# A four-layer model on one core: score constants built on many rows at once, the first search's preparations stepped inside it, layer 2's combine paced, and layer 3's weights loaded during layer 2

## The chip, the cores and the metric

The kernel runs on one core of a Trainium2 chip. The metric is the device time of one execution in microseconds (us); lower is better. All arithmetic is in 32-bit floats. The core has TensorE (PE, matrix products into PSUM, with a separate row PEld for its weight loads), VectorE (DVE), ScalarE (ACT), GpSimd (POOL), and SyncE (SP), whose queue issues most DMAs.

## The reference

Input and output are 8 sequences (b) of 512 tokens of 128 numbers. Four layers follow one another; each is an attention-like part and a feed-forward part (ffn), each added to a running x after a normalisation.

- Layer 0: differential attention, 16 heads of 8 with two score maps each (m = 0 and 1), a causal mask and a per-head linear position bias; beside it a mixture of 4 routed experts (2 chosen by a softmax gate) and 2 shared ones.
- Layer 1: softmax attention for the queries whose greatest score stands out most from their mean score, and a routed mixture of many small experts.
- Layer 2: a gated delta rule (a linear attention with a state per head, in blocks of 32 tokens, with short convolutions ahead of it) beside a mixture of experts whose tokens are gathered by expert.
- Layer 3: softmax attention with a relative position bias, beside a gated ffn whose weights come as integers to be divided by 127.

Of layer 0, what the change touches is this:

```python
bias = slopes[None, :, None, None] * pos_diff[None, None, :, :]
causal = jnp.where(jnp.triu(jnp.ones((s, s), bool), 1), -jnp.inf, 0.0)[None, None]
s0 = jnp.einsum('bhqd,bhkd->bhqk', q0, k0) * scale - bias + causal
s1 = jnp.einsum('bhqd,bhkd->bhqk', q1, k1) * scale - bias + causal
w0 = jax.nn.softmax(s0, axis=-1)
w1 = jax.nn.softmax(s1, axis=-1)
```

## The kernel before, in words

**Order.** TensorE's order is written out by hand: the stages are Python generators, and `step(gen)` lets one go on by one yield, `drain` to its end. The order of the other engines' instructions, and of SP's queue, is made by a scheduler that works with simulated times of its own and keeps to the data's dependencies. Every tile belongs to a pool; a tag with `bufs=n` cycles through n buffers, and a new tile waits until the old one's readers are done. A pool that is opened where a closed one lay waits for all of the old one's tiles there.

**Layer 0.** `score_rows` (L377) makes the constant rows of the score product. K and Q tiles `KA[i][m][g]` and `QA[i][m][g]` (two buffers i, for alternating batches; two maps m; four head groups g) have four groups of 32 rows, one per head. In each group rows 0 to 7 are the head's q or k, row 8 is the negated greatest score, and the following rows carry position bias and a causal mask inside a block, so that one product of 32 rows gives the biased score. Before, 18 such rows are built one at a time: a k row for eight heads and a q row, each made by POOL in one of two ping-pong buffers (tags "flat" and "nmT", L402 to L415), scaled by the slope on DVE, and sent by two small DMAs to the DRAM tiles `l0kc` and `l0qc` (L416, L417). From there 20 DMAs fill the master tiles QA[0][0][0] and KA[0][0][g] (L420, L424), and 27 copies on ACT and DVE (L431) fill the others.

`attention0_inputs(b)` (L435) normalises x, transposes it and makes q, k and v; q and k go through the buffers "flat" to DRAM (L452), and `attention0_loads(b, i)` (L461, DMAs L468) brings head pair i back into rows 0 to 7 by 8 DMAs. `gate0` (L612) is the softmax gate, of five steps, whose last writes the weights to DRAM (`wd`, L626) for `ffn0` (L629) to spread over the partitions as C (L636). An ffn step multiplies by the first weights (`ph`), applies ACT, multiplies by C on POOL (L649), and two steps later multiplies by the second weights into `po`; the first addend of `po` is a bias product with the gate's transposed weights. `attention0_greatest(b)` (L472) is the search for each row's greatest score: 8 head pairs of 6 steps (r = 0 to 47); per step, score products into PSUM and DVE's fused reductions (L500); once per pair a transpose (`pmx`, L481), a negation on ACT and a small DMA to row 8. The values (products with exponentiated scores) follow the search.

At the start, `layers01` (L217) drains batch 0's inputs, all its loads, batch 1's inputs and loads, and both gates; then it runs the first search with one ffn step on every odd r (24 steps).

**Layer 2** (`layer2`, L1027). A unit u is one block of 128 tokens of four of the sequences; 8 units in all, each of 12 rounds. In each unit `rounds` interleaves the delta rule's stages on TensorE: `delta_front` (L1403: window copies nb, convolution outputs y, the transposes byt and chan, products), `delta_inverse` (L1489), which makes two products, AT and PT, of 32-column blocks (256 small matmuls on 32 by 32 tiles, then two DVE multiplications by the decay factors E, L1504), and inverts a triangular matrix by repeated products pY and flips TM (L1525); `delta_scan` (L1597) carries the state; `delta_output` (L1637). The experts (`experts2`, L1313) run beside units 0 to 3. From unit 4 on, `combine2` (L1369) goes on by one step per round: for one finished unit at a time it gathers each token's two expert outputs by indirect DMAs that POOL issues (L1311), sums them on DVE (L1384, L1391), adds the delta rule's output and adds the result to x on POOL (L1394). Tiles nb1, y, byt, chan1, AT, TM, Y, gl and E lie in layer 2's own pool `wk`.

**Layer 3** (`layer3`, L1682) opens new pools where layer 2's lay, loads Wv, Wq, Wk, the bias and Wo, scales Wq on POOL (L1692), and transposes three integer weights (`dequantised`, L1909: a DMA, a cast and a scaling on DVE L1917/L1918, three transposes L1921, an evacuation) ahead of the first transposed norm. Then it runs 64 groups of scores (DVE L1784), softmax, values and ffn.

Of the kernel before, what the change touches and what calls it, by code (L numbers as in the profile page):

```python
# [16 lines left out]
P = 128  # L17
# [14 lines left out]
def tile_kernel(ctx: ExitStack, tc: tile.TileContext, w: dict, out: bass.AP):  # L32
# [7 lines left out]
    fw = sm2 = None  # L40
# [176 lines left out]
    def layers01():  # L217

        nonlocal wk
        with ExitStack() as lx:  # L220
# [5 lines left out]
            with tc.manual_schedule(engines={mybir.EngineType.PE}):  # L226
                for b in range(2):
                    drain(attention0_inputs(b, c))
                    for i in range(8):
                        attention0_loads(b, i, c)  # L230
# [3 lines left out]
                drain(gate0(0, c), gate0(1, c))  # L234
                ffn = ffn0(c)
                for r, _ in enumerate(attention0_greatest(0, c)):
                    if r % 2:
                        step(ffn)
                done = iter(())
# [137 lines left out]
    def score_rows(lp, dram):  # L377

        KA, QA = ([[[lp.tile([P, S], F32, name=f"l0{n}A{i}{m}{g}") for g in range(4)] for m in range(2)] for i in range(2)]
                  for n in "kq")
        row = lp.tile([1, H8], F32, name="l0slr")
        for h in range(H8):
            V.memset(row[:, h : h + 1], 2.0 ** (-8.0 * (h + 1) / H8))
        sd = dram.tile([H8, 1], F32, name="l0sd", bufs=1)
        nc.sync.dma_start(sd.rearrange("h o -> o h"), row)
        slope = lp.tile([H8, 1], F32, name="l0slope")  # L390
        nc.sync.dma_start(slope, sd)
        n = 18
        kc = dram.tile([H8, n, S], F32, name="l0kc", bufs=1)
        qc = dram.tile([n, S], F32, name="l0qc", bufs=1)
        for r in range(n):
            t = wk.tile([H8, S], F32, tag="flat", name=f"l0kc{r}")
            q = wk.tile([1, S], F32, tag="nmT", name=f"l0qc{r}")
            if r == 0:
                G.memset(t, 1.0)
                G.memset(q, 0.0)  # L400
            elif r < 5:
                G.iota(t, pattern=[[P, NT], [0, P]], base=-P * (r - 1), channel_multiplier=0, allow_small_or_imprecise_dtypes=True)  # L402
                G.memset(q, 0.0)
                G.memset(q[:, (r - 1) * P : r * P], 1.0)
            elif r == 5:
                G.iota(t, pattern=[[0, NT], [1, P]], base=-64, channel_multiplier=0, allow_small_or_imprecise_dtypes=True)
                G.memset(q, 1.0)
            else:
                k, i = divmod(r - 6, 3)
                G.memset(t, 0.0)  # L410
                G.memset(t[:, k * P + 32 * (i + 1) : k * P + 32 * (i + 2)], 1.0)
                G.memset(q, 0.0)
                G.memset(q[:, k * P : k * P + 32 * (i + 1)], -30000.0)
            if 1 <= r <= 5:
                V.tensor_scalar(t, t, slope, None, ALU.mult)  # L415
            nc.sync.dma_start(kc[:, r, :], t)  # L416
            nc.sync.dma_start(qc[r : r + 1, :], q)  # L417
        V.memset(QA[0][0][0], 0.0)
        for j in range(4):
            nc.sync.dma_start(QA[0][0][0][32 * j + 8 : 32 * j + 8 + n, :], qc)  # L420
        for g in range(4):
            V.memset(KA[0][0][g], 0.0)
            for j in range(4):
                nc.sync.dma_start(KA[0][0][g][32 * j + 8 : 32 * j + 8 + n, :], kc[4 * j + g])  # L424
        at = 0
        for i in range(2):
            for m in range(2):
                for g in range(4):
                    for X, src in ((KA, KA[0][0][g]), (QA, QA[0][0][0])):
                        if X[i][m][g] is not src:  # L430
                            (A.copy, V.tensor_copy)[at % 2](X[i][m][g], src)  # L431
                            at += 1
        return KA, QA, qc[0:1, :].rearrange("o n -> (o n)").partition_broadcast(4)
# [593 lines left out]
    def layer2():  # L1027
        nonlocal wk, fw, sm2
        with ExitStack() as lx:
# [9 lines left out]
            with tc.manual_schedule(engines={mybir.EngineType.PE}):  # L1039
# [4 lines left out]
                out = iter(())  # L1044

                def rounds(u, experts, combined, n_experts):
                    nonlocal out
                    scan = delta_scan(u, c)
                    inverse = delta_inverse(u + 1, c) if u + 1 < N else iter(())
                    front = delta_front(u + 2, c) if u + 2 < N else iter(())  # L1050
                    for r in range(12):
                        step(scan)
                        step(experts)
                        if not u and r > 1:
                            step(experts)
                        step(inverse)
                        if r > 1:
                            step(front)
                        if r % 3 < n_experts:
                            step(experts)  # L1060
                        step(out)
                        if u > 3:
                            step(combined)
                    drain(scan, inverse, front, out)
                    out = delta_output(u, c)
# [10 lines left out]
                with tc.tile_pool(name="ex2", bufs=1) as ep:  # L1076
                    experts = experts2(ep, c)
                    combined = combine2(ep, c)
                    for u in range(1, N):
                        rounds(u, experts, combined, 1)  # L1080
                    drain(out, experts, combined)
# [321 lines left out]
    def delta_front(u, c):  # L1403
# [20 lines left out]
        for back in range(4):  # L1424
            x = wk.tile([P, 4, P], F32, tag=f"nb{back}", name=f"nb{back}{nm}", bufs=1 if back else 4)
# [13 lines left out]
        y = wk.tile([P, 4, S], F32, tag="y", name=f"y{nm}", bufs=1)  # L1439
# [35 lines left out]
        for i, parts in enumerate((((0, None, G), (1, gam, V)), ((0, beta, G), (1, None, V)))):  # L1475
            byt = wk.tile([P, 2, 4, 4, 32], F32, tag="byt", name=f"byt{i}{nm}", bufs=1)
            for k, part in enumerate(parts):
                scaled(byt[:, k], *part)
            x = wk.tile([P, 2, 4, 4, 32], F32, tag=f"chan{i}", name=f"chan{i}{nm}", bufs=1 if i else 3)
# [9 lines left out]
    def delta_inverse(u, c):  # L1489
# [7 lines left out]
        prod = []  # L1497
        for i, n in enumerate(("AT", "PT")):
            pp = psS.tile([P, 4, 4, 32], F32, tag="S", name=f"p{n}{nm}")
            for ch in range(4):  # L1500
                for h in range(4):
                    tiles32(pp[:, ch, h, :], r["KT"][:, ch, h, :], chan[1][:, i, ch, h, :])
            x = wk.tile([P, 16, 32], F32, tag=n, name=f"{n}{nm}", bufs=1 + i)
            V.tensor_tensor(x, pp.rearrange("p c h i -> p (c h) i"), E, ALU.mult)  # L1504
            prod.append(x)
            yield
        AT, r["PT"] = prod
# [15 lines left out]
        def flipped(n):  # L1523
            x = wk.tile([P, 16, 32], F32, tag="TM", name=f"TM{nm}_{n}", bufs=1)
            V.transpose(x.rearrange("p n i -> p (n i)"), TT.rearrange("p n i -> p (n i)"))  # L1525
            return x
# [3 lines left out]
        for n in range(1, 5):  # L1530
# [3 lines left out]
            Y = wk.tile([P, 16, 32], F32, tag="Y", name=f"Y{nm}_{n}", bufs=1)  # L1534
# [51 lines left out]
    def decay_pairs(u, g, c):  # L1586

        gl = wk.tile([P, 16, 32], F32, tag="gl", name=f"gl{u}", bufs=1)
# [3 lines left out]
        E = wk.tile([P, 16, 32], F32, tag="E", name=f"E{u}", bufs=1)  # L1592
# [89 lines left out]
    def layer3():  # L1682
        nonlocal wk
        with ExitStack() as lx:
            lp = lx.enter_context(tc.tile_pool(name="l3", bufs=1))
            wk = lx.enter_context(tc.tile_pool(name="wk3", bufs=2))
            c = dict(lp=lp, xnT={}, v={}, qk={}, P={}, PT={}, th={}, s={})
            for n in "vqk":
                c["w" + n] = loaded(lp, [P, 1024], w[f"L3_attn_W{n}"], f"l3w{n}")
            c["bias"] = position_bias(lp, shared["bias"])  # L1690
            c["wo"] = loaded(lp, [P, 8, D], w["L3_attn_Wo"].rearrange("(g p) o -> p g o", p=P), "l3wo")
            G.tensor_scalar(c["wq"], c["wq"], 1.0 / 64.0, 0.0, ALU.mult, ALU.add)  # L1692
# [7 lines left out]
            c["gT"], c["uT"], c["dT"] = (dequantised(lp, w[f"L3_ffn_w_{n}"], n) for n in ("gate", "up", "down"))  # L1700
# [208 lines left out]
    def dequantised(pool, src, name):  # L1909

        raw = pool.tile([P, 3, P], I32, tag="rawi", name=f"rawi{name}")
        if src.shape[0] == P:
            nc.sync.dma_start(raw, src.rearrange("o (c p) -> o c p", p=P))
        else:
            nc.sync.dma_start(raw, src.rearrange("(c p) d -> p c d", p=P))
        f = pool.tile([P, 3, P], F32, tag="rawf", name=f"rawf{name}")
        V.tensor_copy(f, raw)  # L1917
        V.tensor_scalar(f, f, 1.0 / 127.0, None, ALU.mult)  # L1918
        pt = psS.tile([P, S], F32, tag="S", name=f"pti{name}")
        for k in range(3):  # L1920
            T.transpose(pt[:, k * P : (k + 1) * P], f[:, k, :], ident)  # L1921
        dst = pool.tile([P, 3, P], F32, name=f"l3{name}")
        evac(dst, pt[:, 0 : 3 * P].rearrange("p (c o) -> p c o", o=P))
        return dst

    with tc.tile_pool(name="x12", bufs=1) as x12:
        with tc.tile_pool(name="fw", bufs=8) as fw:
            layers01()
        layer2()
    layer3()  # L1930


# [21 lines left out]
```

## Time and profile before

| | us |
|---|---|
| three timed runs | 4029.34, 4039.8 (median), 4045.39 |
| the profiled execution | 4008.45 |
| its span in the profile | 4006.7 |
| TensorE busy in it | 3580.8 (89%) |
| DVE / ACT / POOL busy | 2268.1 / 1831.8 / 1470.8 |
| mean granted TensorE clock | 0.933 |
| first score product of layer 0 | 69.68 |
| first rhs of the delta rule's units 0 to 7 | 2509.1, 2611.6, 2698.1, 2779.5, 2861.6, 2979.3, 3062.5, 3122.6 |
| last addition to x in layer 2, first softmax input of layer 3 | 3168.61, 3204.72 |

The profile's page and the trace come from one profiled execution; its times run from the span's start. The page gives busy time by engine, the span in 40 slices of about 100 us with each engine's busy tenths, and the TensorE clock that was granted in tenths of full speed. Timelines list runs of like instructions, with the idle time of the engine before them and what ended it in square brackets. The table of waits sums such idle times by what was waited for. The table of windows gives busy time and counts by engine for chosen stretches.

### The profile page before, as it was taken

The numbers are of one execution on the slowest core, as the hardware profiler recorded it, in microseconds if no ns is written. First come the engines' busy times: TensorE is split into PE (matmuls) and PEld (weight loads), VectorE is DVE, ScalarE is ACT, GpSimd is POOL, SyncE is SP. The second block draws the span as 40 slices with busy tenths as digits, with TensorE's granted clock in tenths as the row PEclk, the third lists the DMA queues.
The fourth block names the chain that finished last, engine by engine and source line by source line (L and its number), as shares of the span: only waits on it lengthen the run. The fifth ranks groups of instructions, "written<-read, shape, count | busy, mean of one in ns | idle before, by whom it ended". The sixth has DMA issues, their size and how long they took to land. (4 is left out here: it accounts for less than half of the span.)

```text
span 4006.7 us, 87035 instructions
## 1 busy us (share of the span) xinstructions
PE 3580.8 (89%) x33646; PEld 1712.2 (43%) x33646; DVE 2268.1 (57%) x7301; ACT 1831.8 (46%) x3996; POOL 1470.8 (37%) x2122
## 2 busy tenths in 40 slices
PE   3899999999999999999999985788947599999998
PEld 1343344444344333333333333456635355555555
DVE  4655666665655544446446646544454466666665
ACT  1254454455454556565664641122211155555554
POOL 2233334334443333332333333444373133333333
PEclk6999999999999999999999987899967699999999
DMA  3000000000011232222222320011020200000000
GB/s 110 29 23 30 28 13 30 30 18 26 26 44 51 75 104 72 80 73 72 71 75 68 81 75 28 11 42 51 28 51 22 63 1 4 4 4 4 4 4 6
DMA packets 139420, 163.29 MB, mean 41 GB/s; under 512 B 30047, under 2 KB 79878, under 8 KB 138880
## 3 DMA queue, kind: packets, MB, share of 16 engines
q1 hardware_dynamic: 135680, 150.91, 13.2%
q0 software_dynamic: 3328, 6.82, 1.0%
q8 instruction: 266, 4.36, 0.5%
q14 instruction: 146, 1.20, 0.1%
HBM read 129.94 MB, written 30.08 MB: 40 GB/s over the span
## 5 line engine op out<-in xcount | busy, mean ns | idle before, releaser
L500 DVE CUSTOM_DVE_ANT_0 l0junk<-ps,l0junk 128x512 f32<-128x512 f32 (+3 forms) x1024 | 502.2, 490 | 394.1 <-PE ps L82 319.6
L985 POOL TENSOR_TENSOR h<-h,C 128x512 f32<-128x512 f32 x256 | 325.2, 1271 | 640.1 <-ACT h L983 587.0
L556 ACT ACTIVATE PT<-pt 128x512 f32<-128x512 f32 (+1 forms) x768 | 360.9, 524 | 404.7 <-PE ps L82 364.2
L807 DVE TENSOR_REDUCE nm<-ps 128x1 f32<-128x512 f32 x512 | 331.7, 685 | 327.2 <-PE ps L82 326.2
L1791 POOL TENSOR_SCALAR P<-P,l 128x128 f32<-128x128 f32 (+3 forms) x512 | 262.8, 532 | 537.8 <-DVE l L1789 382.4
L1788 ACT ACTIVATE P<-P,mx 128x128 f32<-128x128 f32 (+3 forms) x512 | 281.2, 550 | 300.0 <-DVE mx L1786 296.5
L82 PE MATMUL ps<-l0kA,l0qA 32*128 32x512 f32 (+3 forms) x2048 | 403.8, 479 | 11.4 <-DVE mx L500 11.4
L560 POOL TENSOR_SCALAR_AFFINE_SELECT PT<-PT 128x256 f32<-128x256 f32 x512 | 202.0, 407 | 518.9 <-ACT PT L556 486.7
L82 PE MATMUL pt<-l0qA,l0kA 32*128 32x512 f32 (+3 forms) x2048 | 373.2, 468 | 2.0 <-DVE nm L807 1.1
L82 PE MATMUL ps<-l1kA,l1qA 32*128 32x512 f32 x1024 | 332.0, 652 | 29.0 <-DVE nm L807 26.7
L845 ACT ACTIVATE PT<-pt 128x512 f32<-128x512 f32 x512 | 276.3, 595 | 176.0 <-PE ps L82 146.3
L82 PE MATMUL av<-PT,vl0v 128*9 128x512 f32 (+3 forms) x3072 | 319.4, 504 | 1.2 <-POOL PT L560 1.2
L82 PE MATMUL ph<-xnT,l1e 128*128 128x512 f32 x512 | 295.4, 660 | 7.2 <-DVE H L834 2.7
L982 ACT ACTIVATE h<-ph 128x512 f32<-128x512 f32 x272 | 162.8, 599 | 252.6 <-PE ph L82 227.0
L82 PE MATMUL pt<-l1qA,l1kA 32*128 32x512 f32 x1024 | 273.6, 644 | 1.0 <-DVE nm L807 1.0
L82 PE MATMUL po<-h,l1e 128*128 128x512 f32 x512 | 266.5, 602 | 0.0
L82 PEld LDWEIGHTS pt<-l0qA,l0kA 32*128 32x128 f32 x2048 | 165.3, 184 | 206.8 <-DVE mx L500 66.9
L1784 DVE CUSTOM_DVE_ANT_0 P<-ps,l3bias 128x128 f32<-128x128 f32 (+3 forms) x512 | 225.0, 486 | 41.2 <-PE ps L82 39.4
L649 POOL TENSOR_TENSOR h<-h,C 128x512 f32<-128x512 f32 x128 | 163.0, 1274 | 112.3 <-ACT h L647 64.3
L647 ACT ACTIVATE h<-ph,l0b 128x512 f32<-128x512 f32 x192 | 132.0, 687 | 127.6 <-PE ph L82 127.5
L82 PEld LDWEIGHTS ps<-l0kA,l0qA 32*128 32x128 f32 x2048 | 158.3, 187 | 48.3 <-DVE mx L500 34.7
L82 PE MATMUL ps<-kT,qT 64*128 64x128 f32 (+3 forms) x1024 | 176.0, 456 | 1.2 <-ACT kT L77 0.7
(522 smaller groups left out, 6424.5 us busy)
## 6 DMA issues: line engine op xcount, KB each, us to landing
C<-wd SPq DMA_DIRECT2D x288, 256.0 KB
qd<-qf SPq DMA_DIRECT2D x24, 256.0 KB
kd<-kf SPq DMA_DIRECT2D x24, 256.0 KB
l0qA<-qd SPq DMA_DIRECT2D x256, 16.0 KB
l0kA<-kd SPq DMA_DIRECT2D x256, 16.0 KB
l2e<-in_L_ffn_w_dram SPq DMA_DIRECT2D x16, 256.0 KB
l3flat<-l3short SPq DMA_DIRECT2D x16, 192.0 KB
l2eo_d<-eo SPq DMA_DIRECT2D x8, 320.0 KB
```

What stands on the lines that cost most here:

```text
L82: T.matmul(out_, lhsT, rhs, start=start, stop=stop)
L500: V.tensor_tensor_reduce(c["junk"][:, : (qb + 1) * P], pss[j][:, at], c["mask"][:, (3 - qb) * P :], 1.0, NEG, ALU.add, ALU.max, mx[i][:, q ...
L556: A.activation(p[:, j % 2, :N], pss[j][:, :N], AF.Exp)
L560: G.affine_select(out=own, in_=own, compare_op=ALU.is_ge, fill=0.0, base=0, pattern=[[0, 2], [1, P]], channel_multiplier=-1)
L649: G.tensor_tensor(h, h, C[b, e], ALU.mult)
L807: V.tensor_reduce(nm[g][:, j, qb : qb + 1], pss[j], AX.X, ALU.max, negate=True)
L845: A.activation(Pt[j // 2][:, j % 2, :], pss[j], AF.Exp)
L982: A.activation(h, ph, AF.Relu)
L985: G.tensor_tensor(h, h, C[b, u - u % 2][:, u % 2, :], ALU.mult)
L1784: V.tensor_tensor_reduce(p, src, c["bias"][:, 2 * g + j, (3 - qb) * P :], 1.0, NEG, ALU.add, ALU.max, mx[:, n : n + 1])
L1788: A.activation(p, p, AF.Exp, bias=mx[:, n : n + 1], accum_out=l[:, n : n + 1])
L1791: G.tensor_scalar(p, p, l[:, n : n + 1], 1.0, ALU.mult, ALU.mult)
```

## The change

Four parts.

(a) `score_rows` now makes 22 constant rows (16 mask rows where there were 12), built on many rows at once with memsets, iotas and affine selects, and sent to DRAM by 7 DMAs. The master tiles are QA[1][1][0] and KA[1][1][g], and the copies go to buffer 0 first.

(b) The start of `layers01` drains only batch 0's inputs and three of its loads. Gate 0, the other five loads, batch 1's inputs, its loads and its gate become steps of the first search, at the values of r that the diff shows; ffn steps run at r of 16 and more, on three of four (again 24).

(c) In layer 2 the combine is stepped on odd rounds only. A pool `wk23` (`wf`), opened below layer 2's pools and kept through layer 3, holds nb1, y, byt, chan1, AT, TM, Y, gl and E. AT and PT come from two halves of 64-column matmuls with four half multiplications.

(d) `weights3` is stepped in unit 7: it loads layer 3's Wv, Wq, Wk, Wo and the three integer weights into those tiles' buffers, scales, casts and transposes them. Layer 3 itself then only loads the bias and bo.

```diff
             with tc.manual_schedule(engines={mybir.EngineType.PE}):
-                for b in range(2):
-                    drain(attention0_inputs(b, c))
-                    for i in range(8):
-                        attention0_loads(b, i, c)
+                drain(attention0_inputs(0, c))
+                for i in range(3):
+                    attention0_loads(0, i, c)
...
-                drain(gate0(0, c), gate0(1, c))
-                ffn = ffn0(c)
+                ffn, gate, inputs, gate_1 = ffn0(c), gate0(0, c), attention0_inputs(1, c), gate0(1, c)
                 for r, _ in enumerate(attention0_greatest(0, c)):
-                    if r % 2:
+                    if r % 3 == 0 and r < 15:
+                        step(gate)
+                    if r % 2 == 0 and r < 10:
+                        attention0_loads(0, 3 + r // 2, c)
+                    if 16 <= r < 24:
+                        step(inputs)
+                    elif r % 2 == 0 and r >= 26 and r < 42:
+                        attention0_loads(1, (r - 26) // 2, c)
+                    if r % 4 == 0 and r >= 28:
+                        step(gate_1)
+                    if r >= 16 and r % 4 != 3:
                         step(ffn)
+                drain(gate, inputs, gate_1)
...
-        n = 18
+        n = 22
...
-        for r in range(n):
-            t = wk.tile([H8, S], F32, tag="flat", name=f"l0kc{r}")
-            q = wk.tile([1, S], F32, tag="nmT", name=f"l0qc{r}")
...
-            nc.sync.dma_start(kc[:, r, :], t)
-            nc.sync.dma_start(qc[r : r + 1, :], q)
...
+        t = wk.tile([H8, S], F32, tag="flat", name="l0kw")
+        G.memset(t, 1.0)
+        kept(t, [[1, S]], -32, -32)
+        kept(t, [[-1, S]], 63, 32)
+        nc.sync.dma_start(kc[:, 6:n, :].rearrange("h r n -> r h n"), bcast(t, 1, H8))
...
+        for i in range(2):
+            iota(two[1 + i], [[-P, 2], [P, NT], [0, P]], -2 * P * i)
+            V.tensor_scalar(two[1 + i], two[1 + i], slope, None, ALU.mult)
+            nc.sync.dma_start(kc[:, 1 + 2 * i : 3 + 2 * i, :], two[1 + i])
...
+                weights = weights3()
...
-                        if u > 3:
+                        if u > 3 and r % 2:
                             step(combined)
+                        if u == N - 1:
+                            step(weights)
...
-                    drain(out, experts, combined)
+                    drain(out, experts, combined, weights)
...
+        AT = wf.tile([P, 16, 32], F32, tag="AT", name=f"AT{nm}")
+        r["PT"] = wk.tile([P, 16, 32], F32, tag="PT", name=f"PT{nm}", bufs=2)
+        for half in range(2):
+            pp = psS.tile([P, 8, 2, 32], F32, tag="S", name=f"pAP{nm}_{half}")
+            for n in range(8):
+                ch, h = divmod(8 * half + n, 4)
+                tiles32(pp[:, n, :, :], r["KT"][:, ch, h, :], chan[1][:, :, ch, h, :])
+            at = slice(8 * half, 8 * half + 8)
+            for i, x in enumerate((AT, r["PT"])):
+                V.tensor_tensor(x[:, at, :], pp[:, :, i, :], E[:, at, :], ALU.mult)
+            yield
...
+    def weights3():
+        c = shared["w3"] = {}
+        two = wf.tile([P, 2, 1024], F32, tag="y", name="l3wvq")
+        c["wv"], c["wq"] = two[:, 0, :], two[:, 1, :]
+        c["wk"] = wf.tile([P, 1024], F32, tag="byt", name="l3wk")
+        for n in "vqk":
+            nc.sync.dma_start(c["w" + n], w[f"L3_attn_W{n}"])
+        c["wo"] = loaded(wf, [P, 8, D], w["L3_attn_Wo"].rearrange("(g p) o -> p g o", p=P), "l3wo", tag="chan1")
...
+        yield
+        G.tensor_scalar(c["wq"], c["wq"], 1.0 / 64.0, 0.0, ALU.mult, ALU.add)
+        for _ in range(3):
+            yield
+        for raw, (n, key, _, tag) in zip(raws, names):
+            V.tensor_copy(raw, raw.bitcast(I32))
+            V.tensor_scalar(raw, raw, 1.0 / 127.0, None, ALU.mult)
+            yield
...
-        layer2()
-    layer3()
+        with tc.tile_pool(name="wk23", bufs=1) as wf:
+            layer2()
+            layer3()
```

## The prediction

> **What bounds the kernel now.** I read the page's busy shares first, then its 40 slices (the TensorE row and its clock row), because the change touches only a few stages of a 4007 us span.
>
> ```profile
> span 4006.7 us, 87035 instructions
> ...
> PE   3899999999999999999999985788947599999998
> ...
> PEclk6999999999999999999999987899967699999999
> ```
>
> TensorE (PE) is at nine tenths or more almost everywhere. What is left lies in the first slices (0 to 200 us), in slices 24 to 32 (2400 to 3200 us), and nowhere else. The table of windows agrees: from 200 to 2390 us TensorE has 2104.71 of 2190 us. Three views then show the three places.
>
> Start, TensorE's timeline (columns: start, busy, engine, line, what, in brackets the idle time before it and its releaser):
>
> ```profile
> 44.56 2.08 PE L82 MATMUL pq<-xnT,l0wq 128*128 128x512 f32 x2 [11.30 <-ACT qf L448]
> ...
> 69.68 2.80 PE L82 MATMUL ps<-l0kA,l0qA 32*128 32x512 f32 x8
> ...
> 83.90 2.07 PE L82 MATMUL po<-wT,l0b 6*128 6x512 f32 x2
> 114.12 2.07 PE L82 MATMUL po<-h,l0r 128*128 128x512 f32 x2 [28.15 <-POOL h L649]
> ```
>
> The first scores start at 69.68, and at 85.97 TensorE stops for 28 us, for a product of GpSimd (POOL). The table of waits from 30 to 126 us says what POOL wanted: "POOL h L649 <- DMA C<-wd: 42.8". SP's timeline says why C is late: the gate's row wd is sent at 107.74, behind batch 1's eight loads (85.63 to 107.7), 64 DMAs of about 0.33 us each.
>
> Layer 2's valley, busy time and granted clock by windows, and two waits from 2897 to 2998:
>
> ```profile
> 2850.00:2900.00 50.00, 44.83 (x1352) 35.55 (x1353) 27.55 (x78) 13.01 (x32) 20.86 (x26) 0.90 0.10 29
> 2900.00:2950.00 50.00, 23.73 (x584) 14.66 (x582) 20.30 (x49) 4.76 (x12) 40.51 (x47) 0.72 0.28 71
> 2950.00:3000.00 50.00, 22.80 (x840) 16.78 (x840) 31.53 (x74) 6.21 (x12) 38.75 (x37) 0.57 0.26 31
> ```
> ```profile
> DVE g L1384 <- DMA g<-l2eo_d,l2row: 28.1, 7, 6.6
> ...
> PE pY L82 <- DVE TM L1525: 20.5, 2, 12.7
> ```
>
> The first four numbers after the length are PE, weight loads, VectorE (DVE) and ScalarE (ACT), the fifth is POOL. Before the valley PE has 45 of 50 us; in it PE has 23 and POOL 40. POOL issues gathers (L1311) back to back, one per 1.25 us; DVE stands in its queue behind combine's wait for their data, and the delta rule's flips (TM) stand behind that on DVE.
>
> Layer 2 to 3, table of waits from 3168 to 3206:
>
> ```profile
> PE ptigate L1921 <- DVE rawfgate L1918: 24.0, 1, 24.0
> ```
>
> Layer 3's transposes of a weight that was only requested at 3178.35 stand ahead of its first norm in PE's order. The last x is ready at 3168.61, the first softmax input is read (L1784) at 3204.72: 36.1 us.
>
> **Start, constants.** Removed: 36 row DMAs of 0.22 to 0.45 us that SP issues from 14.48 to 44.40 among others, and the POOL/DMA ping-pong over two buffers, which also holds qf (ACT idle 13.24 us, "<-POOL l0kc L410"). Added: 7 DMAs, about 7 × 0.3 = 2 us of SP, and a dozen POOL and DVE operations of 1 us or less (estimate from POOL's 0.4 us L560 select on 256 columns). The slope's round trip stays (requested 14.08 and 18.43), so kc is there about 23 and the 20 master loads (1.36 + 5.65 us of SP) issue by about 31. The 27 copies of about 0.53 us on two engines remain (7.4 us), and the instruction order puts them ahead of batch 0's first xnT evacuation: projections at 33 to 40, at half clock (1.04 us each matmul of 512). Only three of eight loads (8 DMAs, 2.6 us each) precede the first scores: about 46 instead of 69.68.
>
> **Start, search.** Full-clock rows of 120 to 192 give a head pair: PE 1.07+1.65+1.37 scores, 0.44 transpose, about 0.2 of gaps: 4.75 us; an ffn step 1.92; DVE 9.7 (6 × 0.69 and its smaller forms, 16 reductions of 0.08). Steps 0 to 15 are 2.67 pairs without ffn, so DVE is the bound: 2.67 × 9.7 = 26, plus 3 for the gate's small DVE work: to 75. Steps 16 to 47: 5.33 × 4.75 = 25.3; 24 ffn steps × 1.92 = 46.1; batch 1's inputs 5.3; its gate and bits 2.8: 79.5. Moved with the gate: its wd and C DMAs; at about step 13 they pass loads 3 to 7 (40 DMAs, 13 us of SP, spread over 26), but C stands behind one search row and one qd store on SP, each waiting for work of steps 16 to 18. I put 5 us there, the length of such a round trip by Wq's 5.1 us from issue to use, and 3.5 for clock steps. End: 75 + 79.5 + 8.5 = 163. Before, values start at 192.2. **Gain 28**, bounds 18 (C waits twice as long and first scores 5 later) and 36 (neither stall).
>
> **Clock, row against rule.** The windows give 69.68 to 85.97: PE 16.09 of 16.29 us busy at a granted clock of 0.50, whereas 114.12 to 120.00, 5.88 us busy, was followed by 0.99. My 79.5 us are at full clock. The Trainium skill (TensorE: Matmul & The Clock Gate, What's actually happening) says that one busy window of about 3.4 us releases the clock. By that rule all 79.5 us run full; by the first row they may not. The row disagrees with the rule, the second agrees, and the difference is the third rival's price.
>
> **Layer 1 to 2.** The first bias load now waits for s1sb of batch 7 (2403) where it waited for PE at 2390; its norm at 2409.4 stays. 0 to 1 us lost.
>
> **Layer 2, products.** pAT and pPT were 256 matmuls of 32 columns a unit; pY's 128 such take 1.25 us, so 2.5. Now 128 of 64 columns; 32 of those take 0.47 (pu), so 1.88: 0.6 us × 8 = 5, minus four DVE halves in place of two products of 0.69 (about +0.3 a unit), with some issue gaps saved. AT comes one round later. **Gain 4**, 0 to 8.
>
> **Layer 2, pacing.** Combine steps only on odd rounds from unit 4. In the instruction order, 22 gathers still stand in one row on POOL right after unit 5's decay product gl. But until unit 7's window copies (nb) POOL now has 48 gathers and 12 x-additions instead of 56 and 16: 8 × 1.25 + 4 × 0.42 = 11.7 us less. These come later, over unit 7, where POOL is 14 of 50 to 68 us busy, with 4 us of new stall. **Gain 8**, 0 (the row of 22 is what stalls) to 40 (of the valley's 50 us of PE stalls, 12.69 + 10.12 + 7.82 + 3.65 + the rest, all but the gather waits' ends go).
>
> **Layer 3's weights.** Four loads and three raw ones, about 4.9 us of SP, move into unit 7, behind unit 4's expert sum loads and ahead of unit 5's s store: none waits there for anything unfinished. POOL's scaling (1.07 us) waits for Wq: 5.1 us from issue to use at 3168.64, behind it unit 6's and 7's Vb and state. Plus six DVE operations of 0.36, three evacuations of 0.5, nine transposes (2.7). Unit 7's PE is 38 of 68 us busy, so part hides. **Cost 2**, 0 to 6 (the whole Wq wait uncovered).
>
> **Boundary.** Gone from PE's order ahead of ptxnT: the 24.0 us wait and three transposes. What is late next: xn, which DVE writes at 3172.95 to 3173.88, behind four bias memsets of 0.91 (their buffer, a new pool's, still waits for layer 2's last addition). So ptxnT ends about 3174.4 and not 3191.9. The bias load (3170.06 plus 2.88) lands about 3177 and is wanted about 3187. **Gain 17.5**, 14 to 20. Layer 3 and layers 0 and 1 after 200 us keep their work.
>
> **Sum**: 28 − 1 + 4 + 8 − 2 + 17.5 = 54.5 on a profiled execution of 4008.45 us (span 4006.7). The three timed runs have a median of 4039.8, 31.4 above it; none of the edits touches what differs, so the difference counts from there: 4039.8 − 55 = **3985**.
>
> **Rivals.**
> (1) *The valley opens.* For: every stall there ends in DVE or POOL work behind a gather. Against: 22 gathers stay in a row. Gain 32 more: about 3953. Chance 0.12.
> (2) *The start pays half and the valley nothing*: ffn waits for C again, now behind the search's rows on SP, as it waited before. Gain 18 (start) + 3 (products) + 15 (boundary) − 4 (weights) = 32: 4008. Chance 0.17.
> (3) *The clock stays at 0.50 through steps 16 to 47*, for its row above, against the rows from 120 on. The 79.5 us then take 159: search ends at 242, 50 later than before. With 15 from the boundary, 4 from the products, nothing in the valley and 4 for the weights: 4039.8 + 50 − 15 = 4075, slower. Without it the start gains 28 and these 15: it decides once 43 of the 79.5 us (54%) run at half clock. Chance 0.05.
> (4) *The change doesn't do what it says*: the planner's order puts the loads, gathers and weights so that each wait only moves (first scores still near 70, the first layer 3 input still 36 us after x). About 4030. Chance 0.08.
> My forecast keeps 0.58, spread 3965 to 4003.
>
> A measurement here tells about 0.5% (20 us) from no change. Faster by more: forecast, (1) and (2), 0.87 less the tail of (2) near 4020: 0.85. Within: (4) and part of (2): 0.11. Slower: (3) less its mild part: 0.04. The range takes the forecast, (2) and most of (1): 3948 to 4014.
>
> **What would show it.** In the profile after: first scores near 46; TensorE without an idle time of 20 us or more before 150, with clock 1.0 from about 80; values from about 163; combined products in 1.9 us a unit at full clock; units 4 to 6 of layer 2 shorter by 8 in sum while POOL's row of gathers remains; softmax input about 18 us after the last x. The prediction is wrong if C's wait ends later than 90 us, if Wq's scaling delays a state in unit 7 by more than 6 us, or if stages outside these move.

## The result, and the profile after

The changed kernel takes 3981.95 us (median of four runs, 3977.89 to 3987.41) beside 4034.66 for the kernel before: ratio 0.9867, 95% interval 0.984 to 0.9894, or 53 us less. The forecast was 3985. Its profiled execution is one of the four runs (3987.41 us, span 3985.7). Times of runs below are medians; one run of the kernel before (4648.91) and one of warm_all (6557.68), far above all others of their kernel, are not counted.

The two profiled executions differ by only 21 us of span, though, not 53. From the two traces, stage by stage (us from the first to the next mark):

| stage | before | after |
|---|---|---|
| to layer 0's first scores | 69.7 | 47.0 |
| first scores to first values (the search) | 122.5 | 126.4 |
| values to the end of layer 1 | 2197.6 | 2202.3 |
| end of layer 1 to layer 2's first rhs | 119.3 | 124.3 |
| first rhs of unit 0 to that of unit 7 | 613.5 | 619.1 |
| unit 7 to the last combine sum | 43.6 | 43.7 |
| last combine sum to layer 3's first softmax input | 38.5 | 21.3 |
| rest | 802.0 | 801.5 |

So the boundary did what was forecast (17 us), the start gave 18.8 us up to the values where 28 were forecast, and layer 2, whose terms were to bring 12 us, looks 6 us longer. Either the change loses there, or the trace of before is not typical. That was the first question for the experiments.

Page of the profile after:

```profile
span 3985.7 us, 84887 instructions
...
PE   5999999999999999999999975689957699999998
...
PEclk7999999999999999999999987789967799999999
```

Counted from 0, slice 0 has risen from 3 to 5 and slice 31, with the boundary in it, from 5 to 6; layer 2 (slices 24 to 31) still holds the low figures. 2148 instructions are gone, almost all of them by the merged products (1024 matmuls and as many weight loads).

TensorE's timeline of the start after:

```profile
47.00 2.35 PE L82 MATMUL ps<-l0kA,l0qA 32*128 32x512 f32 x4 [5.80 <-DMA l0kA<-kd]
...
51.08 14.44 PE L82 MATMUL ps<-l0kA,l0qA 32*128 32x512 f32 x52
...
78.16 2.08 PE L82 MATMUL ph<-xnT,l0r 128*128 128x512 f32 x2
...
94.95 2.07 PE L82 MATMUL po<-h,l0r 128*128 128x512 f32 x2 [4.22 <-POOL h L669]
```

First scores at 47.0 (forecast 46), the 28 us wait for C down to 4.22 (forecast 5). But from 47 on, four windows (length, then busy time of PE, weight loads, DVE, ACT, POOL, then the granted clock) show another cost:

```profile
47.00:78.00 31.00, 30.84 (x112) 17.41 (x112) 22.25 (x91) 1.39 (x3) 0.98 (x4) 0.50 0.20 57
78.00:90.70 12.70, 12.70 (x24) 4.22 (x22) 6.37 (x29) 3.24 (x5) 0.00 (x0) 0.55 0.06 23
94.95:107.40 12.45, 12.45 (x22) 4.13 (x22) 3.82 (x13) 1.28 (x2) 2.39 (x2) 0.54 0.15 52
107.40:173.00 65.60, 64.71 (x269) 26.32 (x269) 38.16 (x155) 17.95 (x28) 17.42 (x17) 1.00 0.15 41
```

TensorE is busy for all but 0.2 of 43.7 us at a granted clock of 0.50 to 0.55. The boundary, from the table of waits from 3162 to 3206, has lost the 24.0 us wait for a weight to be transposed; what is left is a wait for the first norm:

```profile
PE ptxnT L125 <- DVE xn L118: 12.8, 1, 12.8
```

### The profile page after: what moved, and what is told of

The parts are those of the page before. It is cut to its first block, busy times and chain, and to the rows that moved or that the text cites. A ratio compares the mean times of both kernels' runs of the same rounds, so it can differ in the third digit from the quotient of the medians.

```text
span 3985.7 us, 84887 instructions
## 1 busy us (share of the span) xinstructions
PE 3612.3 (91%) x32622; PEld 1727.2 (43%) x32622; DVE 2261.6 (57%) x7315; ACT 1832.8 (46%) x3996; POOL 1459.5 (37%) x2072
## 4 chain that ended last, share of the span: by engine, by line
PE 75%; DVE 12%; issue 4%; POOL 3%; ACT 3%; DMA 1%; SPq 1%; POOLq 0%; DVEq 0%; ACTq 0%
PE ph L82 12%; PE pt L82 12%; PE po L82 10%; PE av L82 10%; PE ps L82 7%; PE ptp L1819 3%; PE py L82 3%; PE pk L82 2%; PE s L82 2%; PE pq L82 2%; ACT P L1806 2%; PE pv L82 2%; PE pY L82 1%; DVE P L1802 1%; PE pU L82 1%
## 5 line engine op out<-in xcount | busy, mean ns | idle before, releaser
L82 PE MATMUL ps<-l0kA,l0qA 32*128 32x128 f32 (+3 forms) x2048 | 421.0, 489 | 16.7 <-DVE mx L520 10.7
L82 PEld LDWEIGHTS ps<-l0kA,l0qA 32*128 32x128 f32 x2048 | 166.6, 191 | 58.6 <-DVE mx L520 38.2
L82 PE MATMUL av<-PT,v 128*64 128x128 f32 (+3 forms) x1024 | 173.1, 445 | 4.3 <-ACT PT L77 2.5
```

The costliest lines, as they stand in the source:

```text
L82: T.matmul(out_, lhsT, rhs, start=start, stop=stop)
```

## The experiments

All twelve are the kernel before or after with parts taken, left or added; every kernel was timed against the kernel before on its chip.

**control: before, unchanged.**

> The kernel before, unchanged, for a second profiled execution and more times. Theory 1: the first profiled execution (4008.45 us) was a lucky one, 21 to 37 us below its timed runs, and what differs lies in one or two stages (layer 2's valley and its clock, most likely). Then this profile's span is 4028 to 4045 us, and its first rhs of layer 2 and last x come 20 to 35 us later than 2509 and 3169. Theory 2: the profile lengthens or shortens nothing and stages scatter evenly; then the span is anywhere in 4005 to 4045 with no stage standing out. Ratio to before 0.998 to 1.002 in both.

4037.5 us, ratio 0.9996 (0.9987 to 1.0004); span 4038.9. Theory 1 holds, except that layer 2's first rhs comes only 6 us later than in the first trace (2515.2), not 20 to 35; the last x comes 32 later. Units 0 to 7 (from the first rhs of unit 0 to that of unit 7) take 639.8 us here, and 636.8 to 641.8 in the four other traces with the old combine and products (start_only, boundary_only, consts_only, steps_only), against 613.5 in the first trace. So the trace that the prediction worked from was 26 us short in layer 2 alone. TensorE's rows of the tables of waits over units 0 to 7 show the form that it takes. The first trace of before:

```profile
PE pu L82 <- DVE rhs L1612: 24.8, 6, 10.1
PE pY L82 <- DVE TM L1525: 22.1, 5, 12.7
PE pU L82 <- issue: 16.7, 14, 2.1
...
PE pY L82 <- issue: 7.2, 4, 2.3
```

and control:

```profile
PE pY L82 <- issue: 35.5, 52, 2.0
PE pU L82 <- issue: 24.8, 42, 2.1
...
PE pY L82 <- DVE TM L1525: 10.2, 3, 8.6
```

"issue" is idle time in which the engine waited for nothing that the profile shows. Summed over all of TensorE's rows it is 59.5 us in the first trace and 99.7 to 113.1 in those five. Why one execution escaped it stays open.

**start_only: the constants and the steps.**

> Only the constants and the stepped start, layers 2 and 3 as before. By the stage marks of the two traces the start gives 18.8 us (values from 173.4 in place of 192.2). Theory 1 (the start's gain stays whole up to the end): 16 to 21 us faster than before, about 4014 beside 4034. Theory 2 (a part is given back later, as the two traces had 4 us less of it at the end of layer 1 and 9 less at layer 2's first unit): 8 to 14 us faster.

4019.43 us, ratio 0.9948 (0.9934 to 0.9962): 21 us. Theory 1: the start's gain lasts to the end. Values start at 175.1, 16.5 before control's 191.6.

**consts_only and steps_only: its halves.**

consts_only makes, of the whole change, only the edits in `score_rows`, from

```diff
-        n = 18
+        n = 22
```

to the copies; steps_only makes only those in `layers01`, from

```diff
-                for b in range(2):
-                    drain(attention0_inputs(b, c))
-                    for i in range(8):
-                        attention0_loads(b, i, c)
+                drain(attention0_inputs(0, c))
+                for i in range(3):
+                    attention0_loads(0, i, c)
```

to the drain after the search.

> Only the constant rows made on many rows at once, the rest as before (both batches' inputs, loads and gates ahead of the search). Theory 1: the constants take away the first stage alone; first scores 10 to 16 us earlier (56 in place of 70, still behind eight loads and both gates), and since batch 1's loads still fill SP's queue ahead of the gate's row, the wait for C moves along: 8 to 14 us faster at the start of the values. Rival: nothing is left of it, as C still waits for SP, within 4 us of before.

> Only the loads, gates and second inputs as steps of the search, with the constant rows made one at a time as before. Theory 1: the first scores come at about 61 (three loads in place of eight and no gates ahead), no 28 us wait for C but one of about 4, and steps 0 to 15 at half clock: values 5 to 10 us earlier than before. With the run before it makes the start's 19 to 20.

0.9981 (0.9971 to 0.999) and 0.9989 (0.9979 to 0.9998): about 8 and 4 us, 12 in all where both together give 21. Values start at 185.3 and 186.3, 6.3 and 5.3 before control's: theory 1 of steps_only holds, that of consts_only falls short (8 to 14). The first scores come at 60.2 and 59.7. Each half leaves a long wait that the other would remove. In consts_only, C still stands behind batch 1's loads (the last is sent at 98.7, C at 101.8); in steps_only, batch 0's loads stand behind the old rows and the master tiles that come after them (sent up to 52.3). One row of TensorE's timeline from each, consts_only first:

```profile
106.81 2.07 PE L82 MATMUL po<-h,l0r 128*128 128x512 f32 x2 [30.32 <-POOL h L660]
```
```profile
59.74 2.28 PE L82 MATMUL ps<-l0kA,l0qA 32*128 32x512 f32 x4 [30.96 <-DMA l0kA<-kd]
```

**boundary_only: layer 3's weights in unit 7.**

> Only layer 3's weights loaded in unit 7 into tiles that outlive layer 2; start, combine and products as before. Theory 1: 17 us faster (first softmax input 21 us after the last addition to x in place of 36 to 38), units unchanged. Rival: the weights' DMAs, scaling and transposes lengthen unit 7 by 5 us or more, and only about 10 are left.

4023.79 us, ratio 0.9961 (0.9948 to 0.9974): 16 us. From the last combine sum to layer 3's first softmax input it has 22.6 us, control 38.7; units 6 and 7 do not grow (62.2 and 43.9 against control's 62.0 and 43.7). Theory 1, with nothing of the rival to be seen.

**layers23_only: all but the start.**

> The whole change but for the start: paced combine, merged products, layer 3's weights. Theory 1 (my prediction's terms: 8 valley, 4 products, 15 boundary): 25 to 30 us faster. Theory 2 (what the two traces show: layer 2 from its first rhs to its last 6 us longer, boundary 17 shorter): 8 to 14 us faster. With the start run, the sum should make the whole change's 53.

4005.2 us, ratio 0.9916 (0.9903 to 0.9929): 34 us, more than either theory. Less the boundary's 16, layer 2's two edits bring 18. Units 0 to 7 take 619.6. With the start's 21 it makes 55 beside the whole change's 53: the parts add up.

**no_pace and no_merge: layer 2's edits one by one.**

Both start from the whole change. no_pace:

```diff
-                        if u > 3 and r % 2:
+                        if u > 3:
```

no_merge has the two products again, each with one multiplication by E:

```diff
-                tiles32(pp[:, n, :, :], r["KT"][:, ch, h, :], chan[1][:, :, ch, h, :])
...
+                    tiles32(pp[:, ch, h, :], r["KT"][:, ch, h, :], chan[1][:, i, ch, h, :])
```

> The whole change, but the combine is stepped on every round again. In the runs so far unit 4 took 125 to 127 us with the old pace and products and 120 to 121 with the new, unit 5 87 to 88 and 79. Theory 1 (the pacing did it): units 4 and 5 go back to about 126 and 87, the kernel 12 to 15 us slower than the whole change, units 0 to 3 unchanged. Theory 2 (the merged products did it, by fewer instructions on TensorE and an earlier PT): they stay at 120 and 79.

> The whole change, but AT and PT come from two products of 32 columns again. My prediction's term: 4 us slower than the whole change, 0.6 us in every unit. Theory 2 (the merge made units 4 and 5 shorter): 12 us or more slower, in units 4 and 5.

3995.87 and 3995.74 us, ratios 0.9893 (0.9875 to 0.9911) and 0.9892 (0.9875 to 0.991). On the same chip warm_gap, the next kernel (the whole change but for a small edit at the start that is worth 2.5 us in its trace), has 3980.4. Taking either away costs some 13 us beyond that edit, as theory 1 of no_pace and theory 2 of no_merge have it. But each of these gives one edit alone the credit for units 4 and 5, and both have a part: unit 4 takes 125.4 us without the pacing and 123.7 without the merge (120.2 with both), unit 5 83.2 and 84.8 (79.2). Units 0 to 7 in us:

| | combine every round | combine on odd rounds |
|---|---|---|
| products apart | 636.8 to 641.8 (five traces) | 637.0 |
| products merged | 629.6 | 617.5 to 625.3 (four traces) |

The merge alone is worth about 10 (one trace), the pacing alone 0 to 5 (one trace, within the scatter of the five), both together 12 to 24, and 18 by the timed runs.

**warm_gap and warm_all: what holds the clock.** Both add products into a PSUM tile that nothing reads; the last two lines, in the search, are warm_all's alone.

```diff
+                def warm(k, n):
+                    pp = psS.tile([P, S], F32, tag="S", name=f"warm{k}")
+                    for _ in range(n):
+                        mm(pp, c["wq0"], c["xnT"][0])
...
+                warm("g", 6)
...
+                    if r < 16:
+                        warm(r, 1)
```

> The whole change, and six products of 128 rows by 512 columns into an unused PSUM tile ahead of the first scores, where TensorE waits 5.8 us for a load; nothing reads them. In the trace the granted clock is 1.00 until that wait and 0.50 from 47 to 106 us, although TensorE is busy all of it. Theory 1 (the wait drops the clock, and score products of 32 rows cannot lift it, but keep it): steps 0 to 15 run at 1.00, first ffn step at about 73, search ends 8 to 14 us earlier. Theory 2 (32-row products do not even keep it): the clock falls to 0.50 a few us after 47 and at most 3 us are gained. Theory 3 (something outside TensorE's work sets it): no difference.

> As the run before, and one such unused product more in each of steps 0 to 15 (16 times 0.86 us of work that nothing needs). Theory 1 of the run before: the clock is held there too, and this one is equal or up to 3 us slower than it, since DVE bounds those steps. Theory 2 (full-height products are needed to keep the clock): here alone the clock stays at 1.00 from 47 on, and the search ends 8 to 14 us earlier than in the whole change.

Windows of the start, warm_gap:

```profile
51.00:55.00 4.00, 2.66 (x11) 0.98 (x7) 3.68 (x20) 0.21 (x1) 0.64 (x2) 1.00 0.46 135
55.00:60.00 5.00, 4.65 (x16) 3.17 (x18) 4.10 (x19) 0.00 (x0) 0.22 (x1) 0.63 0.41 117
60.00:70.00 10.00, 10.00 (x38) 4.53 (x36) 8.13 (x35) 0.59 (x1) 0.02 (x1) 0.50 0.21 45
```

and warm_all:

```profile
55.00:60.00 5.00, 5.00 (x20) 1.77 (x18) 3.66 (x19) 0.00 (x0) 0.00 (x0) 1.00 0.34 91
60.00:70.00 10.00, 10.00 (x42) 3.48 (x40) 7.47 (x31) 0.59 (x1) 0.00 (x0) 1.00 0.18 46
...
88.00:98.00 10.00, 5.09 (x10) 1.25 (x9) 0.00 (x0) 0.69 (x1) 3.70 (x3) 0.64 0.39 130
```

In warm_gap the clock is 1.00 when the scores begin and 0.50 some 9 us later, at 56.3. That alone does not tell products of few rows from waiting, since TensorE also waits in between: it is busy only 2.66 of 4 us from 51 to 55. On the steps of 3.41 us in which the granted clock changes in these traces it reads:

```profile
49.49:52.90 3.41, 3.26 (x26) 1.78 (x25) 2.73 (x15) 0.21 (x1) 0.00 (x0) 1.00 0.21 49
52.90:56.31 3.41, 1.87 (x6) 0.88 (x6) 3.07 (x18) 0.00 (x0) 0.86 (x3) 1.00 0.79 249
56.31:59.73 3.42, 3.42 (x13) 2.42 (x13) 2.67 (x13) 0.00 (x0) 0.00 (x0) 0.50 0.21 49
```

The first step holds little but score products of 32 rows, and the clock stays; the second holds 1.54 us of waits, and the clock falls. From 56.3 to 73.4 TensorE is busy throughout, mostly with such products, and the clock stays at 0.50. In warm_all one product of 128 rows beside each step's scores adds work and fills the waits, and the clock is 1.00 until the wait for C. So theory 2 has the effect right (the clock falls, 2.5 us gained in warm_gap's values), but that products of 32 rows cannot hold or lift a clock is not shown, and the whole change's own trace has a counterexample: from 1222.58 to 1225.99 score products of 32 rows, up to four side by side, are all that TensorE runs, and the clock rises.

```profile
1222.58:1225.99 3.41, 3.41 (x14) 2.04 (x16) 2.45 (x5) 1.08 (x2) 0.26 (x1) 0.50 0.01 4
1225.99:1229.40 3.41, 3.41 (x34) 1.74 (x31) 2.14 (x5) 1.85 (x4) 0.55 (x2) 1.00 0.00 0
```

warm_all gained less than theory 2 said. Its values start at 171.9, because some 14 us of unused products and the wait for C eat what the clock gives, and its 3999.57 us (0.9909) are 19 above warm_gap's though its values come 1.0 later; by its trace 9 more go between the values and the end of layer 1 (2205.1 us; the other traces scatter from 2195.9 to 2206.3) and 8 in layer 2's units 0 to 7, for which I have no cause.

**early_p3 and early_nofill: a version that draws on these.** Against the whole change, early_p3 (with the function `warm` above):

```diff
+                warm("g", 6)
...
+                step(gate)
...
+                    if r < 9:
+                        warm(r, 1)
-                    if r % 3 == 0 and r < 15:
+                    if r % 2 == 0 and r < 8:
                         step(gate)
...
-                    if 16 <= r < 24:
+                    if 18 <= r < 26:
                         step(inputs)
...
-                    if r >= 16 and r % 4 != 3:
+                    if r >= 9 and (r - 9) * 24 // 39 != (r - 8) * 24 // 39:
                         step(ffn)
...
-                        if u > 3 and r % 2:
+                        if u > 3 and r % 3 == 1:
```

early_nofill leaves both calls of `warm` out.

> A version that draws on the runs so far. Start: six unused products in the wait ahead of the first scores and one in each of steps 0 to 8 (nothing reads them), the gate's steps at once and its row sent before batch 1's inputs, the 24 ffn steps spread over steps 9 to 47. Layer 2: the combine on every third round. Theory 1 (the start is bounded by TensorE's work once the clock is held and C comes early): from 47 on 38 us of scores, 46 of ffn and 8 of inputs and gate remain, so values start at 142 to 152 in place of 173, no wait for C. Rival (C still comes late, the clock falls again): 165 or later. Layer 2: units 4 to 6 within 5 us of the whole change's 120, 79 and 59, since a row of 22 gathers still stands on POOL; a longer tail after unit 7 is the risk. Whole kernel about 3955 to 3962.

> As the version before (early gate, ffn steps over 9 to 47, combine on every third round), without the unused products. Theory 1 (full-height products hold the clock, the wait ahead of the first scores loses it): 0.50 from 47 on, as in the whole change, until the ffn steps that begin about 62 lift it, some 10 to 25 us later; values at 157 to 166 in place of 152, the kernel 5 to 14 us slower than with the unused products, and still faster than the whole change. Rival (the clock hardly matters, C's earlier row made all of the gain): values at 150 to 154.

early_p3: 3958.16 us, ratio 0.9798 (0.9784 to 0.9812), 80 us faster than before, and by the two ratios 28 faster than the whole change. Its start, by windows:

```profile
47.00:60.00 13.00, 12.97 (x51) 4.94 (x52) 9.26 (x40) 0.22 (x1) 0.87 (x3) 1.00 0.35 100
60.00:70.00 10.00, 10.00 (x47) 3.66 (x48) 7.51 (x28) 0.64 (x2) 0.12 (x1) 1.00 0.17 42
70.00:90.00 20.00, 19.49 (x81) 7.20 (x82) 12.51 (x50) 5.25 (x8) 7.51 (x6) 1.00 0.27 78
```

Full clock, no wait for C, values at 152.0 in place of 173.4. Unit 4 of layer 2 takes 111.8 us (119.6 to 120.9 in the four traces with odd rounds), so the combine on every third round is worth some 9 more in that unit, where I had expected at most 5. early_nofill: 3958.38, ratio 0.9806 (0.9788 to 0.9824). Its clock is 0.50 from 48 to 85 us and its values start at 157.5, at the lower end of theory 1, but the whole kernel isn't measurably slower (theory 1 said 5 to 14 us): the 5.5 us that the unused products give at the start do not stand out from the scatter of the rest. They can be left out.

## Why the prediction was right

The time, the sign and the order of the parts came out. Two terms were wrong by 7 and by 6 us, in opposite directions: that the total is within 3 us is partly luck. Term by term, forecast and measured:

- **Constants and first scores**: 46, measured 47.0. Right.
- **C's wait**: 5 us, measured 4.22 on TensorE, at the place named: C is sent at 89.73, right behind a qd store that SP could not send before 88.82. The length was right, the time was not: the wait ends at 94.95, past the 90 us that the prediction named as a sign of being wrong, most likely because the steps ahead of it ran at half clock. Values start at 173.4, not 163, and the clock is 1.00 through the rest of the search from 106 on, not from about 80.
- **Steps 0 to 15**: 29 us, "so DVE is the bound". Measured 31.2, but DVE, priced at 26 and 3 more, is busy 22.25 of 31.00 us and TensorE 30.84: TensorE at half clock was the bound. Right size, wrong engine.
- **The failed term: "3.5 for clock steps" in steps 16 to 47.** They took 95.2 us, forecast 88. Of this, 25.15 us (78 to 90.7 and 94.95 to 107.4) ran at 0.50 to 0.55, which costs about 11 to 13 against full clock (an estimate from these clocks; no run takes away just this). The third rival, with its row of 16.09 busy us at 0.50, had the mechanism, for a third of the stage instead of most of it. By the rule of the Trainium skill (TensorE: Matmul & The Clock Gate, What's actually happening), one busy window of 3.4 us releases the clock; the 40 us busy at 0.50 here speak against it, with busy meaning any product. The start gave 21 by the timed runs (18.8 by the first pair of traces), forecast 28, bounds 18 and 36; the prediction's own marks, 192.2 and 163, make 29.
- **Layer 2, pacing 8 and products 4**: 18 measured (34 less 16). The term was mis-sized, and split the wrong way. I priced the merge by TensorE's busy time, 0.6 us a unit, and that part came out: over units 0 to 7 the two products are busy 23.7 us in no_merge and the merged one 19.8 in the whole change, 0.56 a unit. What I had only noted as "some issue gaps saved" is larger: TensorE's waits for issue at these products are 12.7 us in no_merge and 3.2 in the whole change. In the traces that are typical, the valley has TensorE waiting for issue (99.7 to 113.1 us over units 0 to 7 with the old products and combine, 110.0 in no_merge, 100.3 in no_pace, 90.4 and 91.8 with both edits). The edits seem to help each other: taking away either costs 13 of the 18. That there are fewer matmuls, and fewer gathers beside them, fits this, but as a reason it is argued and not shown. My valley of stalls behind DVE's TM (22.1 us over units 0 to 7, one of 12.69) was larger in the one execution that I could see than in control (10.2).
- **"None of the edits touches what differs" between the profiled execution (4008.45) and the median (4039.8).** Failed: 26 of the 32 us between the first trace and control's lay in layer 2's units 0 to 7, the stage that two of the edits change. Adding the 31 us to the end gave the right time all the same, since the parts that were measured on typical runs (21, 18, 16) sum to 55 and mine to 54.5. That is luck: the start's shortfall and layer 2's surplus cancel.
- **Weights and boundary**: 17.5 less 2, measured 16. Right; the transposed norm waits for xn, as named, the softmax input comes 19 us after the last x (forecast about 18), and unit 7 does not grow (43.7 us to the last combine sum, control 43.7).
- **Layer 1 to 2**: 0 to 1 us lost, for the load that waits longer. The stage took 124.0 to 125.5 us in the seven traces with merged products and 119.3 to 123.3 in the seven with the products apart, among them 120.1 and 119.5 with the changed pools (boundary_only, no_merge). So the pools cost nothing that can be seen, and the merge costs some 3 to 4 us ahead of unit 0, where AT comes a round later (the likely reason, not tested); I had netted that at nothing.

## What to carry to other kernels

Compare the profiled execution with the timed runs before building on its stalls: where it lies outside them, find the stage that differs, or take a second trace, before pricing an edit there. Two preparations that hide one another (a chain of small DMAs, and a row queued behind other rows) are worth little alone and much together: undo both before judging either. A stage of products that use few rows can run at half clock though TensorE is busy: look at the clock beside the busy time, and put work of full height that is needed anyway beside such a stage and into the gap ahead of it. Unused products held the clock here, but brought nothing that the kernel's time shows.

## What the runs showed of the hardware that I had not expected

The granted clock did not follow TensorE's busy time: 0.50 through 40 us of nearly unbroken work, mostly score products of 32 rows, and 1.00 from the first score on where one product of 128 rows stood beside each step. Over all fourteen traces it follows how much of the array the products use. Take the steps of 3.41 us, count the columns that each product streams, and weight them by its rows out of 128, in groups of 32 (a column of a 32-row product counts a quarter). Of the 5209 steps in which every product has 128 weight columns, all with more than 1570 such columns are followed by a clock of 1.00 and all with fewer than 1500 by 0.50, whatever the clock was before. The steps named above fit: in warm_gap 1775 from 49.49 on (the clock stays) and 329 from 52.90 on (it falls), in the whole change 1405 from 51.81 on (it stays at 0.50) and 1910 from 85.94 on (it rises); the rise after 1222.58, with 1556, lies at the edge. This is read from the traces afterwards; no run was made to test it, and for products with fewer weight columns the same count does not separate the steps.

While POOL issues gathers, TensorE can stand for issue. TensorE's timeline of the whole change, one block of 128 products, beside gathers at 1.25 us from 2889.9 to 2909:

```profile
2889.41 0.66 PE L82 MATMUL pY<-TM,AO 32*32 32x32 f32 x53
...
2902.79 0.21 PE L82 MATMUL pY<-TM,AO 32*32 32x32 f32 x1 [1.20 <-issue]
2904.21 0.21 PE L82 MATMUL pY<-TM,AO 32*32 32x32 f32 x1 [1.22 <-issue]
2905.61 0.26 PE L82 MATMUL pY<-TM,AO 32*32 32x32 f32 x2 [1.19 <-issue]
...
2912.72 0.56 PE L82 MATMUL pY<-TM,AO 32*32 32x32 f32 x22 [1.11 <-issue]
```

The records of this stretch add up to all 128, so none is missing: a block that takes 2 us took 24, after its first 53 one to six matmuls at a time, up to 3 us behind the last gather. In control such a row (2911.12 to 2930.91) goes with such a stretch from 2911.3 to 2933.7. The first trace of before has such a row too, from 2897.21 to 2925.66, with two such blocks beside it that are undisturbed but for one gap of 1.16 us:

```profile
2897.02 2.02 PE L82 MATMUL pY<-TM,AO 32*32 32x32 f32 x128
...
2905.53 1.79 PE L82 MATMUL pU<-TT,Y 32*32 32x32 f32 x125
```

So the gathers alone do not suffice. The Trainium skill (Runtime: NRT & Kernel Launch, Instruction fetch mechanics) says that fetching instructions is hidden by the pace at which they are issued; whether fetching is what fails here, no run tells. The traces record transfers of instructions: one of 16 KB from 2890.93 to 2891.95, the next at 2923.84, and the stretch goes on and ends between the two, so no late transfer is seen to end it (control: one landed at 2915.37, the next began at 2943.40). That the starved stretches and the gathers coincide is shown; the cause is not.
